# A Swin block with a dynamic convolution: channels in groups of 64, image halves on the partition halves, a written-out plan for the order

## The chip, the cores and the metric

The kernel runs on one core of one Trainium2 chip. A core has a matrix engine (TensorE, PE in the profile, with PEld for its weight loads), a vector engine (VectorE, DVE), a scalar engine (ScalarE, ACT), GpSimd (POOL) and SyncE (SP), which here only issues DMAs. Each takes its instructions in a fixed order and waits on semaphores. Work lies in SBUF, 128 partitions; products come out in PSUM, eight banks of 512 float32 a partition. The metric is the device time of one execution in microseconds, as the median of several runs.

## What is computed

Sixteen images of 192 channels and 56 x 56 pixels, all float32, go through a Swin block with shifted windows (7 x 7, shift 3, six heads of 32) and then through a depthwise 3 x 3 convolution whose taps are made from the image's own channel means. The reference, cut:

```python
# layer 0
h = _ln(transpose(x, (0, 2, 3, 1)), norm1_g, norm1_b)
h = roll(h, (-SHIFT, -SHIFT), axis=(1, 2))
win = windows of 7 x 7 tokens of h                       # 64 an image, N = 49 tokens
qkv = win @ qkv_w + qkv_b                                # q scaled by HD ** -0.5
attn = softmax(q @ k.T + bias + mask)                    # by head; the mask at the image's rim
out = (attn @ v) @ proj_w + proj_b
x1 = x + roll(windows put back, (SHIFT, SHIFT))
y = gelu(_ln(x1, norm2_g, norm2_b) @ fc1_w + fc1_b) @ fc2_w + fc2_b
x2 = x1 + y
# layer 1
t = relu(batch_norm(x2.mean(axis=(2, 3)) @ w1.T))
wt = (t @ w2.T + b2) * MASK                              # four of nine taps stay, by image and channel
out = depthwise_conv3x3(x2, wt) + bias
```

## The kernel before, in words

**Layout.** Channels lie on partitions as two halves of 96 (`HF`), so an image is a tile [96, 2, 56, 56], double buffered. A product over 192 channels is two matmuls of 96 rows that add up in PSUM. Single PSUM banks come from a pool of four (`bank`), double ones from a pool of two (`banks`).

**Norms.** For a chunk of eight image rows (448 tokens, `CT`), `norm_first` (L231) multiplies x by a matrix of ones over 192 on TensorE to get the mean on every partition (L238, `n_m`), subtracts it on VectorE (L241) and squares on ScalarE (L243). `norm_second` gets the variance as a second product (L250, `n_v`), the root on ScalarE (L252), the reciprocal on VectorE (L253), the product with x on GpSimd (L255), scale and shift on ScalarE (L257). The first norm of the next image runs beside the network of the present one and fills `xe`.

**Attention**, by rows of eight windows (392 tokens, `UT`). `windows` copies a row into window order on GpSimd (L286). `attention_qk` makes q and k in three products (L297: q of heads 0 to 3, k of heads 0 to 3, both of heads 4 and 5); k goes into block-diagonal tiles `kbd`, `kbd2`, zero outside of the blocks, so that one product gives the scores of four (or two) heads (L345, L352, `sc`). The softmax of four windows takes bias, maximum, subtraction on VectorE (L363 to L367), exp on ScalarE (L370), sum and reciprocal on VectorE (L372, L373), the product on GpSimd (L374, `prob`). `attention_v` makes v by window, once for even and once for odd heads (L390, `pv`; 49 columns of weights, at array column 0 or 64), and VectorE puts it into the block-diagonal `vbd` (L400). `attention_values` turns the probabilities on TensorE (L415, `pt`), copies them on ScalarE (L421, `prt`), multiplies (L426, `po`), projects (L445, `pp`) and adds to x on VectorE (L461).

**Network**, by chunks of 448 tokens: `mlp_first` (L470, `ph`; Gelu on ScalarE, L477), `mlp_second` (L486, `pf`), whose VectorE sum with x (L494) also gives the sums for the means.

**Convolution**: `conv_weights` makes the taps, `conv` the four taps of 96 channels, one on ScalarE (L533) and three on VectorE (L545), and writes the result.

**Order.** Image after image: first the eight rows of windows, beside them the convolution of the image before, then seven chunks of network beside the next image's first norm. Inside of these stages a scheduler orders each engine's instructions.

Of the kernel before, what the change touches and what calls it, by code (L numbers as in the profile page):

```python
# [14 lines left out]
HF = 96  # channels of a half: x and all that is as wide lies as two halves of 96 partitions  # L15
# [5 lines left out]
UT = NWIN * N  # tokens of a row of windows  # L21
EXT = IMG + SHIFT
PW = 64 + N  # partitions of two windows (or heads), the second at 64
CR = 8  # image rows of a chunk of tokens
CT = CR * IMG
NCHUNK = IMG // CR
# [3 lines left out]
NTAP = 4  # of the masked 3x3 taps, those that are kept  # L30
SCALE = HD ** -0.5
EPS = 1e-5
MASKED = -3.0e38


@with_exitstack
def tile_swin_then_dynamic_conv(
# [28 lines left out]
    B = x.shape[0]  # L66
    ctx.enter_context(nc.allow_non_contiguous_dma(reason="parameters, once"))

    const = ctx.enter_context(tc.tile_pool(name="const", bufs=1))
    xpool = ctx.enter_context(tc.tile_pool(name="xpool", bufs=2))  # L70
    wide = ctx.enter_context(tc.tile_pool(name="wide", bufs=2))
    lnp = ctx.enter_context(tc.tile_pool(name="lnp", bufs=2))
    att = ctx.enter_context(tc.tile_pool(name="att", bufs=2))
    small = ctx.enter_context(tc.tile_pool(name="small", bufs=4))
    ps1 = ctx.enter_context(tc.tile_pool(name="ps1", bufs=4, space=bass.MemoryType.PSUM))
    ps2 = ctx.enter_context(tc.tile_pool(name="ps2", bufs=2, space=bass.MemoryType.PSUM))

    def bank(name):
        return ps1.tile([128, 512], F32, tag="bank", name=name)

    def banks(name):
        return ps2.tile([128, 2, 512], F32, tag="banks", name=name)

    def load_x(b):
        t = xpool.tile([HF, 2, IMG, IMG], F32, tag="x", name=f"x_{b}")
        for kc in range(2):
            nc.sync.dma_start(t[:, kc], x[b, kc * HF : (kc + 1) * HF])
        return t

# [1 line left out]
    ident = const.tile([128, 128], F32, tag="ident", name="ident")  # L91
    make_identity(nc, ident)
    ones = const.tile([HF, HF], F32, tag="ones", name="ones")
    nc.vector.memset(ones, 1.0 / DIM)
    eps_t = const.tile([128, 1], F32, tag="eps", name="eps_t")
    nc.vector.memset(eps_t, EPS)

    def halves(src, name):
        t = const.tile([HF, 2], F32, tag=name, name=name)
        nc.scalar.dma_start(t, src.rearrange("(k p) -> p k", p=HF))  # L100
        return t

    def column(src, n, name):
        t = const.tile([n, 1], F32, tag=name, name=name)
        nc.scalar.dma_start(t, src.rearrange("(p o) -> p o", o=1))
        return t

    g1, be1 = halves(norm1_g, "g1"), halves(norm1_b, "be1")
    g2, be2 = halves(norm2_g, "g2"), halves(norm2_b, "be2")
    pb, f2b = halves(proj_b, "pb"), halves(fc2_b, "f2b")  # L110
    cb = halves(conv_bias, "cb")

    # q and k come in three products: q of heads 0-3, k of heads 0-3, and q | k of heads 4-5.
    wqkv = const.tile([HF, 2, 3 * DIM], F32, tag="wqkv", name="wqkv")
    qkv_v = qkv_w.rearrange("(k p) n -> p k n", p=HF)
    for to, lo, n in (
        (0, 0, 128),
        (128, DIM, 128),
        (256, 128, 64),
        (320, DIM + 128, 64),  # L120
        (384, 2 * DIM, DIM),
    ):
        nc.scalar.dma_start(wqkv[:, :, to : to + n], qkv_v[:, :, lo : lo + n])
    wp = const.tile([128, 2, DIM], F32, tag="wp", name="wp")
    nc.scalar.dma_start(wp[:, 0, :], proj_w[0:128, :])
    nc.scalar.dma_start(wp[0:64, 1, :], proj_w[128:DIM, :])
    wf1 = const.tile([HF, 2, HID], F32, tag="wf1", name="wf1")
    nc.scalar.dma_start(wf1, fc1_w.rearrange("(k p) n -> p k n", p=HF))
    wf2 = const.tile([128, NFC, DIM], F32, tag="wf2", name="wf2")
    nc.scalar.dma_start(wf2, fc2_w.rearrange("(f p) n -> p f n", p=128))  # L130
    f1b = const.tile([128, NFC], F32, tag="f1b", name="f1b")
    nc.scalar.dma_start(f1b, fc1_b.rearrange("(f p) -> p f", p=128))

    qkb = const.tile([128, 3], F32, tag="qkb", name="qkb")
    for dst, lo, n in ((0, 0, 128), (1, DIM, 128)):
        nc.scalar.dma_start(
            qkb[0:n, dst : dst + 1], qkv_b[lo : lo + n].rearrange("(p o) -> p o", o=1)
        )
    for part in range(2):
        lo = part * DIM + 128  # L140
        nc.scalar.dma_start(
            qkb[part * 64 : part * 64 + 64, 2:3],
            qkv_b[lo : lo + 64].rearrange("(p o) -> p o", o=1),
        )
    qbs = const.tile([128, 2], F32, tag="qbs", name="qbs")
    nc.vector.tensor_scalar(qbs[:, 0:1], qkb[:, 0:1], SCALE, None, ALU.mult)
    nc.vector.tensor_scalar(qbs[0:64, 1:2], qkb[0:64, 2:3], SCALE, None, ALU.mult)

    # v's bias as a row: even heads for partitions 0.., odd ones for partitions 64..
    vb = const.tile([PW, HEADS // 2, HD], F32, tag="vb", name="vb")  # L150
    vb_src = qkv_b[2 * DIM : 3 * DIM].rearrange("(o h j d) -> o h j d", o=1, j=2, d=HD)
    for j in range(2):
        nc.gpsimd.dma_start(
            vb[j * 64 : j * 64 + N], vb_src[:, :, j, :].broadcast_to([N, HEADS // 2, HD])
        )

    # Relative position bias of a pair of windows [q, h, k], with the shift's masks: by row of
    # windows (last or not) and pair in it (last or not).
    rel_r = wide.tile([PW, N, HEADS], F32, tag="wide", name="rel_r")
    nc.vector.memset(rel_r, 0.0)  # L160
    mask_t = lnp.tile([PW, 2, 2, N], F32, tag="sq", name="mask_t")
    nc.scalar.dma_start(mask_t, win_mask)
    # Reversed, the keys of a query are its rows and columns in the table, from its own on.
    side = 2 * WS - 1
    for j in range(2):
        for yq in range(WS):
            q = j * 64 + yq * WS
            nc.sync.dma_start(
                rel_r[q : q + WS].rearrange("p (y x) h -> p y (x h)", y=WS),
                bass.AP(  # L170
                    rel_bias.tensor,
                    yq * side * HEADS,
                    [[HEADS, WS], [side * HEADS, WS], [1, WS * HEADS]],
                ),
            )
    bias_t = const.tile([PW, 2, 2, HEADS, N], F32, tag="bias_t", name="bias_t")
    rel_hk = rel_r[:, ::-1, :].rearrange("p k h -> p h k")
    for r in range(2):
        for e in range(2):
            cut = mask_t[:, r, e, :].rearrange("p (o k) -> p o k", o=1)  # L180
            nc.vector.tensor_tensor(
                bias_t[:, r, e], rel_hk, cut.broadcast_to([PW, HEADS, N]), ALU.add
            )

    # The second layer's small network, with its weights transposed.
    w1n = lnp.tile([RED, DIM], F32, tag="rs", name="w1n")
    nc.scalar.dma_start(w1n, w1)
    w2n = wide.tile([HF, 2, NTAP, RED], F32, tag="wide", name="w2n")
    w2v = w2.rearrange("(k p t) r -> k p t r", k=2, t=9)
    b2t = const.tile([HF, 2, NTAP], F32, tag="b2t", name="b2t")  # L190
    b2v = b2.rearrange("(k p t) -> k p t", k=2, t=9)
    for kc in range(2):
        nc.scalar.dma_start(w2n[:, kc], w2v[kc, :, 0:NTAP, :])
        nc.scalar.dma_start(b2t[:, kc], b2v[kc, :, 0:NTAP])
    w1t = const.tile([HF, 2, RED], F32, tag="w1t", name="w1t")
    w2t = const.tile([RED, 2, NTAP, HF], F32, tag="w2t", name="w2t")
    for kc in range(2):
        pt = bank(f"w1p_{kc}")
        nc.tensor.transpose(pt[:HF, :RED], w1n[:, kc * HF : (kc + 1) * HF], ident[:RED, :RED])
        nc.vector.tensor_copy(w1t[:, kc, :], pt[:HF, :RED])  # L200
        pt = bank(f"w2p_{kc}")
        for t in range(NTAP):
            nc.tensor.transpose(
                pt[:RED, t * HF : (t + 1) * HF], w2n[:, kc, t, :], ident[:HF, :HF]
            )
        nc.vector.tensor_copy(
            w2t[:, kc].rearrange("p t c -> p (t c)"), pt[:RED, : NTAP * HF]
        )
# [17 lines left out]
    for t in [kbd, kbd2, vbd] + prob:  # L226
        nc.gpsimd.memset(t, 0.0)
# [179 lines left out]
    def attention_values(b, u, xt):  # L407
# [46 lines left out]
        if first + WS > IMG:  # L454
            runs.append((IMG - first, WS, 0))
# [230 lines left out]
```

## Time and profile before

| | us |
|---|---|
| runs of the kernel before | 7340.72, 7382.33, 7485.24 |
| their median | 7382.33 |
| span of the profiled execution | 7461.3 |

The profiled execution lies 1.1% over the median. The page gives the busy time of each engine, the span in 40 slices (a digit is a busy share in tenths; the row PEclk is the clock that TensorE was granted, in tenths of full), the DMA queues, the chain of work that ended last, and the costliest groups of instructions. A row of groups reads: line, engine, operation, result<-inputs, shapes, count | busy time, mean ns of one | idle time of the engine just before them, and what ended it. A float32 product stands in it as two records for each matmul of the code. The span and the two engines beside TensorE that the change loads most:

```profile
DVE  4434444344444444444444443444434444344442
ACT  2241422414223142331423314233242331413313
POOL 2111111111111010110101111111011110111100
```

Each image is a stretch of some 464 us, in which about 295 us are attention and 170 us network; ACT's larger digits are the network's Gelu.

### The profile page before, as it was taken

To read this page: it belongs to the slowest core of one execution; us is meant where nothing else is said; L and a number is where in the kernel's file an instruction comes from. 1 tells how busy PE (TensorE), PEld (TensorE's weight loads), DVE (VectorE), ACT (ScalarE), POOL (GpSimd) and SP (SyncE) were. 2 spreads that over 40 slices of the span, in tenths; PEclk is the share of its full clock that TensorE was granted. 3 is DMA by queue.
4 is the path that set the end of the run, shared out by engine and by line. 5 is a ranking of instruction groups with operands and counts; after the bars stand their busy time and mean duration, and the time that the engine had idled before them with its cause. 6 is when DMAs were issued, how large, how long until landed. Compare 5 with 4: busy or idle time off the path is not lost.

```text
span 7461.3 us, 72447 instructions
## 1 busy us (share of the span) xinstructions
PE 6817.7 (91%) x30026; PEld 3549.4 (48%) x30026; DVE 3170.6 (42%) x5505; ACT 2282.5 (31%) x3394; POOL 1044.7 (14%) x1007
## 2 busy tenths in 40 slices
PE   6998989989899898999989989899898998989987
PEld 3445444454444544445444454544544445444443
DVE  4434444344444444444444443444434444344442
ACT  2241422414223142331423314233242331413313
POOL 2111111111111010110101111111011110111100
PEclk8796967869678696786967869587695876958768
DMA  1000000000000000000000000000000000000000
GB/s 38 1 1 26 1 27 1 1 26 1 26 1 2 25 0 27 1 7 20 0 27 1 7 20 0 27 1 7 20 0 26 1 7 20 0 26 1 7 7 13
DMA packets 14171, 83.92 MB, mean 11 GB/s; under 512 B 5603, under 2 KB 7492, under 8 KB 7698
## 3 DMA queue, kind: packets, MB, share of 16 engines
q1 hardware_dynamic: 7952, 77.19, 3.8%
q8 instruction: 236, 3.87, 0.2%
q10 hardware_dynamic: 5826, 2.06, 0.1%
q14 instruction: 93, 0.76, 0.0%
q0 software_dynamic: 64, 0.04, 0.0%
HBM read 40.74 MB, written 38.54 MB: 11 GB/s over the span
## 4 chain that ended last, share of the span: by engine, by line
PE 83%; DVE 7%; ACT 6%; POOL 2%; issue 1%; DMA 0%; ACTq 0%; DVEq 0%; POOLq 0%
PE ph L470 14%; PE pf L486 13%; PE pp L445 9%; PE sc L345 9%; PE pv L390 8%; PE po L426 6%; PE sc L352 5%; PE n_v L250 4%; PE pt L415 4%; PE n_m L238 3%; PE pq L297 3%; PE pk L297 3%; PE pe L297 2%; DVE vbd L400 2%; ACT prt L421 2%; DVE n_rs L253 1%
## 5 line engine op out<-in xcount | busy, mean ns | idle before, releaser
L253 DVE RECIPROCAL n_rs<-n_rs 96x448 f32<-96x448 f32 x224 | 648.0, 2926 | 1022.4 <-ACT n_rs L252 1021.9
L470 PE MATMUL ph<-yn,wf 96*128 96x448 f32 x2688 | 1043.4, 542 | 35.9 <-ACT yn L257 35.9
L486 PE MATMUL pf<-hid,wf 128*96 128x448 f32 x2688 | 1049.8, 539 | 1.6 <-DVE x L494 1.6
L426 PE MATMUL po<-prt,vbd 113*64 113x49 f32 x6144 | 537.9, 301 | 323.6 <-ACT prt L421 318.7
L470 PEld LDWEIGHTS ph<-yn,wf 96*128 96x128 f32 x2688 | 509.4, 190 | 553.6 <-issue 473.1
L255 POOL TENSOR_TENSOR n_xc<-n_xc,n_rs 96x896 f32<-96x896 f32 x224 | 466.1, 2081 | 2029.5 <-DVE n_rs L253 2029.5
L390 PE MATMUL pv<-wqkv,win 96*49 96x96 f32 x8192 | 723.6, 328 | 0.0
L345 PE MATMUL sc<-kbd,q 128*64 128x196 f32 (+1 forms) x2048 | 721.1, 444 | 1.7
L445 PE MATMUL pp<-o,wp 128*96 128x392 f32 (+1 forms) x1024 | 709.8, 817 | 0.0
L486 PEld LDWEIGHTS pf<-hid,wf 128*96 128x96 f32 x2688 | 437.8, 163 | 571.5 <-issue 565.3
L461 DVE SCALAR_TENSOR_TENSOR x<-pp,pb,x 96x371 f32<-96x371 f32 (+2 forms) x576 | 187.8, 387 | 1217.1 <-PE pp L445 1217.1
L426 PEld LDWEIGHTS po<-prt,vbd 113*64 113x64 f32 x6144 | 462.4, 204 | 447.3 <-ACT prt L421 432.4
L390 PEld LDWEIGHTS pv<-wqkv,win 96*49 96x49 f32 x8192 | 600.5, 172 | 91.9 <-issue 75.9
L477 ACT ACTIVATE hid<-ph,f1b 128x448 f32<-128x448 f32 x672 | 424.1, 633 | 590.5 <-PE ph L470 590.2
L400 DVE TENSOR_TENSOR vbd<-pv,vb 49x96 f32<-49x96 f32 x2048 | 522.3, 255 | 128.3 <-PE pv L390 92.0
L363 DVE TENSOR_TENSOR e<-sc,bias_t 113x588 f32<-113x588 f32 x256 | 197.3, 771 | 885.9 <-PE sc L352 885.9
L286 POOL COPY win<-xe 96x392 f32<-96x392 f32 x256 | 171.5, 691 | 2841.4 <-PE pv L390 2837.4
L374 POOL TENSOR_TENSOR prob<-e,tot 113x588 f32<-113x588 f32 x256 | 344.4, 1348 | 1345.5 <-DVE tot L373 1338.7
L370 ACT ACTIVATE e<-e 113x588 f32<-113x588 f32 x256 | 174.9, 689 | 1168.3 <-DVE e L367 1167.0
L415 PE MATMUL pt<-ident,prob 113*128 113x113 f32 x1536 | 371.1, 374 | 173.5 <-ACT kbd L324 69.2
L352 PE MATMUL sc<-kbd,q 64*64 64x98 f32 (+1 forms) x2048 | 476.7, 323 | 1.4 <-ACT kbd L324 1.4
L309 ACT ACTIVATE q<-pq,qbs 128x392 f32<-128x392 f32 x128 | 75.2, 588 | 1192.3 <-PE pq L297 1192.3
(74 smaller groups left out, 6633.6 us busy)
## 6 DMA issues: line engine op xcount, KB each, us to landing
x<-in_x_dram SPq DMA_DIRECT2D x32, 1176.0 KB
out_dram<-y SPq DMA_DIRECT2D x32, 1176.0 KB, 6.3
wf<-in_L_conv_fc_w_dram ACTq DMA_DIRECT2D x2, 576.0 KB, 5.3
rel_r<-in_L_conv_rel_bias_dram SPq DMA_DIRECT2D x14, 8.0 KB
wqkv<-in_L_conv_qkv_w_dram ACTq DMA_DIRECT2D x2, 96.0 KB
wqkv<-in_L_conv_qkv_w_dram ACTq DMA_DIRECT2D x1, 144.0 KB
w2n<-in_L_conv_w_dram ACTq DMA_DIRECT2D x2, 72.0 KB
wqkv<-in_L_conv_qkv_w_dram ACTq DMA_DIRECT2D x2, 48.0 KB, 2.2
```

Source lines behind the costliest of these rows:

```text
L253: nc.vector.reciprocal(rs, rs)
L255: nc.gpsimd.tensor_tensor(xc, xc, rb, ALU.mult)
L297: nc.tensor.matmul(pq[:, :UT], wqkv[:, kc, i * 128 : (i + 1) * 128], win[:, kc].rearrange("p w t -> p (w t)"), start=(kc == 0), stop=(kc = ...
L345: nc.tensor.matmul(sc[rows_, i, 0 : 4 * N], q4[:, cols], kbd[:, w].rearrange("p h t -> p (h t)"), start=True, stop=True,)
L352: nc.tensor.matmul(sc[rows_, i, 4 * N : 6 * N], q2[:, cols], kbd2[:, w].rearrange("p h t -> p (h t)"), start=True, stop=True,)
L390: nc.tensor.matmul(pv[j * 64 : j * 64 + N, i * HF : (i + 1) * HF], win[:, kc, half * 4 + i, :], wv[kc][:, :, j, :], start=(kc == 0), stop= ...
L400: nc.vector.tensor_tensor(vbd[p, half * 4 + i, :, j * HD : (j + 1) * HD], pv[p, i * HF : (i + 1) * HF].rearrange("p (h d) -> p h d", d=HD) ...
L415: nc.tensor.transpose(pt[:, hp * PW : (hp + 1) * PW], pr[:, pair % 2, 2 * hp : 2 * hp + 2, :].rearrange("p h k -> p (h k)"), ident[:PW, :PW],)
L426: nc.tensor.matmul(o[(hp % 2) * 64 : (hp % 2) * 64 + 64, w * N : (w + 1) * N], vbd[:, w, hp, :], prt[:, hp * PW + s * 64 : hp * PW + s * 6 ...
L445: nc.tensor.matmul(pp[:HF, m, :UT], wp[:n, kc, mc], t.rearrange("p r w c -> p (r w c)"), start=(kc == 0), stop=(kc == 1),)
L470: nc.tensor.matmul(ph[:, :CT], wf1[:, kc, f * 128 : (f + 1) * 128], yn[:, kc, :], start=(kc == 0), stop=(kc == 1),)
L486: nc.tensor.matmul(po[:HF, m, :CT], wf2[:, f, m * HF : (m + 1) * HF], hid[:, f, :], start=(f == 0), stop=(f == NFC - 1),)
```

## The change

The kernel is written anew; the reference computation stays.

**Layout.** Channels come in three groups of 64 (`G`), and the partition halves hold two halves of the image: image rows 3 to 30 on partitions 0 to 63, rows 31 to 55 and then 0 to 2 on 64 to 127. Three image tiles [128, 3, 29, 56] take turns. A **round** is one row of windows in each half: 784 tokens; an image has four (`NU`), all images 64 (`S`). A matmul names the part of the array that it uses (`tile_position`): the two halves as row tiles of 64 (q and k, first layer), as column tiles of 64 (second layer, projection of heads 0 to 3), or as four tiles of 64 x 64 (scores, values, the rest of the projection), eight of 64 x 32 (weighted values), four of 128 x 32 (statistics).

**Norms.** Scale and shift of both norms are folded into the weights once, at the start, and so is the subtraction of the mean. What stays by token is 1 over the deviation: x and its square are added over the three groups on GpSimd (`fold`), a product with `blk` gives mean and mean square (`deviations`), and ln and exp(-0.5 ln) on ScalarE take the place of root and reciprocal. The row goes through DRAM to all partitions (one DMA out, two DMAs back for each norm), and GpSimd multiplies (`scaled1` into window order, `scaled2`).

**Attention.** VectorE writes k twice with a mask instead of into blocks. The softmax works on three groups of 16 x 49: VectorE adds the bias and takes maximum, sum and reciprocal, GpSimd subtracts and multiplies, ScalarE takes exp. VectorE turns the probabilities in 32 x 32 blocks, and 24 DMAs a round, all issued by SP, set the blocks in place (`turn_shares`). v comes with all heads at once and is copied by ScalarE; the bias of v is folded into the projection's.

**Network**: as before on 784 tokens; ScalarE changes its function table twice a round.

**Order.** Every operation is recorded with its engine, a duration, and what it reads and writes (`Plan.add`). TensorE's operations stay as recorded; `Plan.order` sets the others by a list schedule with these durations (a DMA's issue counts 0.1, its landing 2 to 4), and the program is put out in that order, each engine waiting for what it needs. PSUM is four double banks in turn (`bank`).

```diff
@@ the order of TensorE's work
+    for r in range(-2, S + 2):
...
+        if has(r + 2) and r > -2:
+            statistics(0, r + 2)
+        if has(r):
+            scores(r)
+        if has(r - 1):
+            weighted(r - 1)
+        if has(r):
+            turn_shares()
+            values(r, (0,))
...
+        if has(r - 1):
+            projection(r - 1)
+            statistics(1, r - 1)
+        if has(r):
+            values(r, (1,))
+        if has(r - 2):
+            second_layer(r - 2, (0, 1))
...
+        if norms:
+            deviations(norms)
+        if has(r + 2):
+            scaled1(r + 2)
+        if has(r - 1):
+            scaled2(r - 1)
+        if has(r - 2):
+            second_layer(r - 2, (2,))
+        if has(r + 1):
+            queries_keys(r + 1)
...
+        if has(r - 1):
+            table("gelu_and_others")
+            first_layer(r - 1)
+            table("natural_log_exp_and_others")
...
+    with tc.manual_schedule():
+        for i in plan.order():
+            plan.ops[i][2]()
@@ statistics and deviations
+            def go(src=src, f=f):
+                nc.gpsimd.tensor_tensor(f, src[:, 0], src[:, 1], ALU.add)
+            def go2(src=src, f=f):
+                nc.gpsimd.tensor_tensor(f, f, src[:, 2], ALU.add)
+            add("POOL", 1.0, go, keys, [("f", n, k)])
+            add("POOL", 1.0, go2, keys + [("f", n, k)], [("f", n, k)])
...
+            for k in range(2):
+                for n in norms:
+                    for h in range(2):
+                        c = 64 * n + 32 * h
+                        nc.tensor.matmul(
+                            p[c : c + 32, k, 0:HT],
+                            blk,
+                            fold[:, n, k, h * HT : (h + 1) * HT],
+                            start=True,
+                            stop=True,
+                            tile_position=(0, c),
+                        )
+
...
+        def away():
+            lo, hi = 4 * norms[0], 4 * norms[-1] + 4
+            nc.sync.dma_start(d[lo:hi], rs[lanes][::16])
...
+        for n in norms:
+            for ab in range(2):
+                def go(n=n, ab=ab):
+                    src = dv[n, ab].rearrange("(o h) t -> o h t", o=1)
+                    nc.sync.dma_start(
+                        rb[n][P(ab)].rearrange("p (h t) -> p h t", h=2),
+                        src.broadcast_to([64, 2, HT]),
+                    )
+                add("SP", 0.1, go, [dk], [("rb", n, ab)], lag=2.2)
@@ a product in two row tiles (q, k; the first layer has wf1, xs2)
+                for g in range(G):
+                    for ab in range(2):
+                        nc.tensor.matmul(
+                            p[:, ab, 0:UT],
+                            lhs_qk(ab, g, i),
+                            d[P(ab), g, 0:UT],
+                            start=(g == 0),
+                            stop=(g == G - 1),
+                            tile_position=(64 * ab, 0),
+                        )
@@ the softmax of a group and the turn
+            def less(j=j, ev=ev):
+                nc.gpsimd.tensor_tensor(
+                    ev, ev, top[j].broadcast_to([128, 16, N]), ALU.subtract
+                )
...
+            def share(j=j, ev=ev):
+                nc.gpsimd.tensor_tensor(ev, ev, tot[j].broadcast_to([128, 16, N]), ALU.mult)
...
+                def turn(kb=kb, e=e, t=t):
+                    nc.vector.transpose(t[:, kb], e[:, :, kb * TL : (kb + 1) * TL])
+                add("DVE", 0.7, turn, [("e", j), "epad"], [("t", ti, kb)])
+            for kb in range(2):
+                for w in range(2):
+                    for qb in range(2):
+                        def go(kb=kb, w=w, qb=qb, t=t, j=j):
+                            n = TL if kb == 0 else N - TL
+                            to, of = 64 * w + TL * kb, 64 * w + TL * qb
+                            nc.sync.dma_start(pt_t[j][to : to + n, qb], t[of : of + n, kb])
@@ weighted values, second layer
+                            nc.tensor.matmul(
+                                p[lane : lane + TL, w, at : at + 64],
+                                v[P(w), ab, pair, h * HD : (h + 1) * HD],
+                                pt_t[j][P(w), :, slot, :],
+                                start=True,
+                                stop=True,
+                                tile_position=(64 * w, lane),
+                            )
...
+                for f in range(NFC):
+                    for ab in range(2):
+                        nc.tensor.matmul(
+                            p[P(ab), i, 0:UT],
+                            wf2[:, f, g * 64 : (g + 1) * 64],
+                            hid[:, f, ab],
+                            start=(f == 0),
+                            stop=(f == NFC - 1),
+                            tile_position=(0, 64 * ab),
+                        )
```

## The prediction

> **What bounds the kernel now.** I read the page from the top: busy shares, the 40 slices, the chain that ended last; then equal stretches of one image, the order of TensorE's work in time, and the costliest groups.
>
> ```profile
> span 7461.3 us, 72447 instructions
> ...
> PE 6817.7 (91%) x30026; PEld 3549.4 (48%) x30026; DVE 3170.6 (42%) x5505; ACT 2282.5 (31%) x3394; POOL 1044.7 (14%) x1007
> ...
> PEclk8796967869678696786967869587695876958768
> ...
> PE 83%; DVE 7%; ACT 6%; POOL 2%; issue 1%; DMA 0%; ACTq 0%; DVEq 0%; POOLq 0%
> ```
>
> TensorE is busy for 91% of the span and carries 83% of the chain; no other engine reaches half. But its clock is granted at 0.777 in the mean. The stretches of one image (columns: stretch, its length, busy PE, PEld, DVE, ACT, POOL with counts, clock, DMA) say where:
>
> ```profile
> 2990.00:3030.00 40.00, 36.78 (x183) 20.48 (x181) 14.26 (x35) 6.37 (x13) 3.86 (x4) 0.54 0.00 1
> ...
> 3150.00:3190.00 40.00, 40.00 (x108) 18.25 (x107) 16.81 (x14) 19.93 (x27) 10.17 (x10) 1.00 0.00 0
> ```
>
> The network runs at 1.00; attention, TensorE just as "busy", at 0.54: its clock is halved for most of it. Two products show what a busy TensorE gets done (columns: start, length, group):
>
> ```profile
> 3127.02 3.17 PE L470 MATMUL ph<-yn,wf 96*128 96x448 f32 x8
> 3130.03 3.17 PE L250 MATMUL n_v<-n_sq,ones 96*96 96x448 f32 x8
> ```
>
> ```profile
> 3057.22 0.91 PE L390 MATMUL pv<-wqkv,win 96*49 96x96 f32 x16
> 3057.96 0.50 PE L345 MATMUL sc<-kbd,q 128*64 128x196 f32 x2
> ```
>
> Each f32 product is two records (1344 `ph` in the code, x2688 in the profile): two passes. Eight `ph` passes of 448 columns take 3.01 us from start to start of the next group: 0.376 us each, **0.84 ns a column and pass** at full clock[...]. Sixteen `pv` passes of 96 columns take 0.74 us, 46 ns each; alone one would take 96 x 0.84 = 81. `pv` puts 49 columns of weights at array column 0 or 64 in turn, so the two column halves work at once.
>
> [...] row tiles and four or eight at once no row of this trace shows. [...] The clock record here holds 1.0 and 0.5 alone. [...] `prob` takes 1.17 us in the median and, once an image, beside the convolution (`y` L545, 3.37 us), this:
>
> ```profile
> 3348.41 4.16 POOL L374 TENSOR_TENSOR prob<-e,tot 113x588 f32<-113x588 f32 x1 [4.51 <-DVE tot L373]
> ```
>
> **The change, part by part.** The unit is now a round: one row of windows in each image half, 784 tokens; 16 x 4 = 64 rounds, plus two before and two after. PE per round, as passes x columns x 0.84 ns / tiles at once:
> - q and k: 36 x 392 / 2 row tiles = 5.9 us. First layer: 72 x 392 / 2 = 11.9. Second: 72 x 392 / 2 column tiles = 11.9.
> - values: 96 x 192 / 4 = 3.9. Projection: 24 x 196 / 4 + 24 x 196 / 2 = 3.0. Statistics: 16 x 196 / 4 = 0.7. Scores: 96 x 98 / 4 = 2.0.
> - weighted: 192 x 64 / 8 = 1.3 if eight tiles keep up; if starts can come no closer than the 40 ns that `pv` and `po` show with two tiles, 192 x 40 = 7.7. I take 2.2: 384 weight loads and passes at the 6 ns that separate the closest starts of two tiles in the trace.
>
> Sum 41.5 us a round, 2,656 us in all. If four and eight tiles do no better than two, values, scores, statistics and the narrow projection double (+7.6) and weighted is 7.7 (+5.5): 54.6. Lower end 40.6.
>
> What goes: the transposes of probabilities on PE (`pt` 371 us) with their copies (`prt`, 224 on ACT), the means over channels as products (`n_m`, `n_v`: 779; statistics is 42 now), the reciprocals and small copies of the next rows:
>
> ```profile
> L253 DVE RECIPROCAL n_rs<-n_rs 96x448 f32<-96x448 f32 x224 | 648.0, 2926 | 1022.4 <-ACT n_rs L252 1021.9
> L255 POOL TENSOR_TENSOR n_xc<-n_xc,n_rs 96x896 f32<-96x896 f32 x224 | 466.1, 2081 | 2029.5 <-DVE n_rs L253 2029.5
> ...
> L400 DVE TENSOR_TENSOR vbd<-pv,vb 49x96 f32<-49x96 f32 x2048 | 522.3, 255 | 128.3 <-PE pv L390 92.0
> L363 DVE TENSOR_TENSOR e<-sc,bias_t 113x588 f32<-113x588 f32 x256 | 197.3, 771 | 885.9 <-PE sc L352 885.9
> ...
> L374 POOL TENSOR_TENSOR prob<-e,tot 113x588 f32<-113x588 f32 x256 | 344.4, 1348 | 1345.5 <-DVE tot L373 1338.7
> ```
>
> The other engines per round, durations scaled by elements from these rows and their like:
> - DVE: three softmax groups of 784 elements (771 ns for 588 gives 0.98; two reductions of 0.96, a reciprocal of 0.22) 9.3; k's blocks 3.3; nine additions of the projection 3.1; second layer 1.8; convolution 4.5 x 0.98 = 4.4; statistics 0.4; six transposes of 512 elements, which no row shows: 0.67 each like a one-input operation of that size, bounds 0.3 and 1.4, so 4.0 (1.8 to 8.4). Sum 26.3.
> - ACT: Gelu 5.5, exponentials 2.6, q and k2 3.3, v and o 3.6, squares 2.3, statistics 1.3, two table loads of 1.28, convolution 1.8. Sum 23.
> - POOL: 2.0 ns an element (`prob`, 1174 for 588) to 2.3 (`n_xc`): six operations of 784 9.4 to 10.9, eight folds of 392 6.3 to 7.3, scalings 5.0 to 5.6. Sum 21 to 24.
> - SP: 24 DMAs of turned probabilities, five for the norms, some 4.5 others: 34, issued 0.3 to 0.5 us apart in the trace's start: 10 to 17.
>
> All lie under 41.5, so they cost only where PE waits. I follow one round from its first score. POOL's subtractions start when the third maximum is taken, at 4.8 us, and its order is then fixed: three subtractions, a share, four folds of norm 2, two shares, four folds of the coming norm 1: 15.7 to 18.2 us, to 20.5 to 23. The statistics product needs the last fold; PE reaches it after 2.0 + 2.2 + 3.9 + 3.0 + 7.9 (two thirds of the second layer) = 19 us. **PE waits 1.5 to 4 us there**; I take 2.5. Queued behind it stand the last third of the second layer, q and k, and the first layer. Second: from statistics to the first layer PE has 4.0 + 5.9 = 9.9 us of cover. The chain there is four small operations, 2.0 with hops, a DMA out, 2.6, two DMAs back, 3 (both landing about 2.2 as `wqkv` does), and one scaling of GpSimd, 0.8: 8.4. It fits if SP is free: on SP the DMA out stands behind up to 23 of the turned probabilities, which end about 24.5 us; just in time. I take 1. Third: in three rounds of four, six convolution steps exclude POOL by turns, at most 6 us, and POOL is late already: 1.5 in the mean.
>
> A round: 41.5 + 2.5 + 1 + 1.5 = 46.5. [...] 62 full rounds: 2,883. The ends: to the first layer of the first round parameters, two norms and one softmax lie bare, about 80; the last two rounds and the convolution (18 x 0.98 on VectorE, writes of 6.3) about 75. Sum 3,038 against the 7461 of the profiled execution; that lies 1% over the median of runs, 7382, so **3,010**.
>
> **Rivals.**
> - All waits are hidden: 41.5 x 62 + 155 = 2,730. For it: every other engine has 15 us to spare. Against: POOL's fixed order.
> - Four and eight tiles work like two (54.6), or [...] the clock halves: attention's 13 us then take 26, and 5 of the network 10. About 55 to 60 us a round: 3,500 to 3,900. For it: attention at 0.54 now.
> - Row halves don't overlap at all: q, k and first layer double (+17.8), values, scores and half the projection too (+7): 66 to 71 a round, 4,300 to 4,600. No row speaks on it.
> - **Slower than before:** SP's DMAs land one by one. 34 x 3.4 us is 116.6, the 7461 / 64 of now: from 3.4 us a DMA on SP is the bound and decides; at 4, 34 x 4 x 64 = 8,700. For it: small transfers here land in 2.2 to 7.7 us, and each waits on SP in order. Against: the instructions wait for the DMA eight before, so eight are in flight and even 7.7 us gives 33 a round.
>
> **The numbers.** Forecast 0.56; all hidden 0.14; two tiles or half clock 0.2; row halves in series 0.06; SP 0.03; no change worth the name 0.01. Range 2,720 to 3,700: it holds the first three but for the end of the third. About 2% is what a measurement here tells from no change. Faster 0.96, same 0.01, slower 0.03.
>
> **What would show it.** Right: PE busy about 90% of 3,000, clock 0.95 or more; first-layer passes starting 165 ns apart in the mean (329 if row halves are in series); 96 value passes within 4 us (8 with two tiles); the statistics product waiting for POOL's folds some 2.5 us, 64 times; `xs2` released by DMA shortly before the first layer. Wrong: PE below 80%, slices of 5 or 6 in the clock row, waits of PE on the turned probabilities or on SP.

## The result, and the profile after

The changed kernel takes **4033.7 us** in the median of four runs (4030.08 to 4042.67), the kernel before 7387.3 in the four runs of that comparison: a ratio of 0.5465, 95% interval 0.5442 to 0.5489. That is far faster, as forecast, but 34% over the predicted 3,010 and 9% over the top of the range. The profiled execution spans 4033.5 us.

The page of the kernel after, its span, busy shares, clock and chain of waits:

```profile
span 4033.5 us, 92760 instructions
...
PE 3006.3 (75%) x40405; PEld 1786.6 (44%) x40405; DVE 1702.7 (42%) x2868; ACT 1401.6 (35%) x1884; POOL 1563.6 (39%) x1427
...
PEclk9888988988988988989889889889889888889888
...
PE 53%; DMA 23%; SPq 9%; DVE 6%; issue 6%; POOL 2%; ACT 1%; DVEq 0%; ACTq 0%; POOLq 0%
```

TensorE is busy for about 3,000 us and idle for 1,000, and it carries 53% of the chain instead of 83%. DMA and SP's queue, nearly absent before, carry 32%. The clock row is 8 and 9 throughout, without the fives and sixes of attention before. Which wait it is, the list of TensorE's waits says (engine, who waited, for what: us in all, times, longest):

```profile
PE ps L738 <- POOL xs L418: 815.7, 64, 18.1
PE ps L656 <- issue: 86.8, 66, 2.4
PE ps L314 <- POOL fold L300: 32.3, 6, 22.2
```

The first layer (L738) waits for the scaling of norm 2 (`xs`, L418) in every one of the 64 rounds, 815.7 / 64 = **12.7 us** in the mean. The statistics product (L314) waits six times in all. One round, in the timeline of TensorE (start, length, group, and the idle time ahead of it):

```profile
1998.34 2.25 PE L508 MATMUL ps<-kbd,q 64*64 64x98 f32 x96
2000.52 1.26 PE L656 MATMUL ps<-pt,v 64*32 64x64 f32 x71
2001.95 1.51 PE L656 MATMUL ps<-pt,v 64*32 64x64 f32 x121 [0.17 <-issue]
2003.40 0.55 PE L619 MATMUL ps<-wqkv,xs 64*64 64x192 f32 x7
2005.42 1.95 PE L619 MATMUL ps<-wqkv,xs 64*64 64x192 f32 x41 [1.48 <-issue]
2007.11 1.26 PE L687 MATMUL ps<-o,wp 64*64 64x196 f32 x24
2008.29 2.21 PE L701 MATMUL ps<-o,wp 128*64 128x196 f32 x24
2010.43 2.18 PE L619 MATMUL ps<-wqkv,xs 64*64 64x192 f32 x48
2012.55 8.12 PE L764 MATMUL ps<-hid,wf 128*64 128x392 f32 x48
2020.60 0.87 PE L314 MATMUL ps<-fold,blk 128*32 128x196 f32 x16
2021.40 4.17 PE L764 MATMUL ps<-hid,wf 128*64 128x392 f32 x24
2025.50 6.20 PE L433 MATMUL ps<-xs,wqkv 64*128 64x392 f32 x36
2043.05 13.92 PE L738 MATMUL ps<-xs,wf 64*128 64x392 f32 x72 [11.35 <-POOL xs L418]
```

From scores to the end of q and k everything runs nearly without a gap: 33.4 us. Then comes the hole of 11.4 us, and the first layer after it takes 13.9 us instead of 11.9: the clock record shows half clock from 2036.5 to 2046.7, and until then pairs of passes start about 0.65 us apart, 0.33 us afterwards. Second layer, q and k and scores take what the prediction gave them to within 0.3 us.

The chain of waits through the same hole (start, length, what; short pieces left out):

```profile
2021.35 0.63 DVE t L579
...
2022.04 0.55 SPq L587
...
2025.87 0.56 SPq L587
...
2026.48 6.70 DMA pt<-t
...
2033.25 4.91 DMA rsd<-rs
...
2038.20 0.67 SPq L369
...
2038.91 2.94 DMA rb<-rsd
...
2041.99 1.02 POOL xs L418
...
2043.05 13.92 PE ps L738 x72
```

Norm 2's factor `rs` (ScalarE, L351, started at 2024.5, 0.37 us) was ready at **2024.85**. Its DMA out (`rsd<-rs`) was issued at 2033.25, **8.4 us later**: on SP it stood behind 23 of the 24 DMAs of turned probabilities (L587, median 588 ns of SP's time each, about 0.62 from start to start). Ten of them were still to be issued when the factor was ready. Near the end SP also stopped twice, 1.5 us in all, until earlier DMAs had landed, because in this program a DMA's semaphore is used again by the eighth DMA after it; the last such landing, which the DMA out itself awaited, came 6.70 us after its issue. The DMA out then took 4.91 until SP could go on, the DMAs back 2.94. From `rs` to the scaling 17.1 us, where the prediction had 5.6 with a free SP.

Of the four kinds of rounds in an image two are like this one. In the other two the DMA out stands behind 15 or 19 of the 24 and starts after 3.5 or 4.9 us, but then the DMAs back are held up longer. In all four the time from `rs` to the scaling is 16.8 to 17.5 us in the mean.

### The profile page after: what moved, and what is told of

It reads as the page before. It is cut to its first block, busy times and chain, and to the rows that moved or that the text cites. A ratio compares the mean times of both kernels' runs of the same rounds, so it can differ in the third digit from the quotient of the medians.

```text
span 4033.5 us, 92760 instructions
## 1 busy us (share of the span) xinstructions
PE 3006.3 (75%) x40405; PEld 1786.6 (44%) x40405; DVE 1702.7 (42%) x2868; ACT 1401.6 (35%) x1884; POOL 1563.6 (39%) x1427
## 3 DMA queue, kind: packets, MB, share of 16 engines
q1 hardware_dynamic: 150722, 185.24, 17.5%
## 4 chain that ended last, share of the span: by engine, by line
PE 53%; DMA 23%; SPq 9%; DVE 6%; issue 6%; POOL 2%; ACT 1%; DVEq 0%; ACTq 0%; POOLq 0%
PE ps L738 23%; DMA pt<-t 12%; PE ps L764 11%; SPq L587 7%; PE ps L619 7%; DMA rb<-rsd 6%; PE ps L656 4%; DMA rsd<-rs 4%; PE ps L508 3%; PE ps L701 3%; DVE y L886 2%; DVE t L579 2%; POOL xs L418 2%; PE ps L687 1%; SPq L369 1%
## 5 line engine op out<-in xcount | busy, mean ns | idle before, releaser
L738 PE MATMUL ps<-xs,wf 64*128 64x392 f32 x4608 | 914.7, 560 | 815.7 <-POOL xs L418 815.7
L738 PEld LDWEIGHTS ps<-xs,wf 64*128 64x128 f32 x4608 | 499.6, 216 | 1230.9 <-POOL xs L418 905.7
L764 PE MATMUL ps<-hid,wf 128*64 128x392 f32 x4608 | 786.4, 495 | 0.0
L750 ACT ACTIVATE hid<-ps,b1f 128x784 f32<-128x784 f32 x384 | 350.6, 913 | 1107.8 <-PE ps L738 1105.1
L549 POOL TENSOR_TENSOR e<-e,top 128x784 f32<-128x784 f32 x192 | 296.8, 1575 | 863.1 <-DVE top L544 863.1
L418 POOL TENSOR_TENSOR xs<-x,rb 128x392 f32<-128x392 f32 x192 | 188.9, 1011 | 1084.9 <-DMA rb<-rsd 1084.9
L764 PEld LDWEIGHTS ps<-hid,wf 128*64 128x64 f32 x4608 | 319.5, 137 | 418.0 <-issue 399.7
L886 DVE SCALAR_TENSOR_TENSOR y<-x,wt,y 128x770 f32<-128x770 f32 x288 | 365.8, 1297 | 270.1 <-ACT y L862 258.4
L567 POOL TENSOR_TENSOR e<-e,tot 128x784 f32<-128x784 f32 x192 | 308.1, 1616 | 260.4 <-DVE tot L562 258.3
L433 PE MATMUL ps<-xs,wqkv 64*128 64x392 f32 x2304 | 398.3, 497 | 5.9 <-POOL xs L400 5.9
L619 PE MATMUL ps<-wqkv,xs 64*64 64x192 f32 x6144 | 313.0, 344 | 28.0 <-issue 28.0
L579 DVE STREAM_TRANSPOSE t<-e 128x512 f32<-128x512 f32 x384 | 254.2, 690 | 66.1 <-DMA pt<-t 60.1
L389 POOL TENSOR_TENSOR xs<-x,rb 128x343 f32<-128x343 f32 x192 | 184.6, 989 | 17.9 <-DMA rb<-rsd 17.9
```

Of the source, the lines that this page charges most:

```text
L418: nc.gpsimd.tensor_tensor(xs2[:, g], xv[:, g], rb[1], ALU.mult)
L433: nc.tensor.matmul(p[:, ab, 0:UT], lhs_qk(ab, g, i), d[P(ab), g, 0:UT], start=(g == 0), stop=(g == G - 1), tile_position=(64 * ab, 0),)
L549: nc.gpsimd.tensor_tensor(ev, ev, top[j].broadcast_to([128, 16, N]), ALU.subtract)
L567: nc.gpsimd.tensor_tensor(ev, ev, tot[j].broadcast_to([128, 16, N]), ALU.mult)
L579: nc.vector.transpose(t[:, kb], e[:, :, kb * TL : (kb + 1) * TL])
L619: nc.tensor.matmul(p[P(w % 2), ab, i * DIM : (i + 1) * DIM], d[P(ab), g, w * N : w * N + 64], wqkv[P(ab), g, 2 * DIM :], start=(g == 0), s ...
```

## The experiments

The variants ran in three batches (A, B, C), each beside the kernel before, whose median was 7373 us in A, 7483 in B and 7478 in C, and 7387 beside the kernel after. Small differences between batches are therefore read from the ratios. The column "wait" is the sum of the list's line for L738 behind L418, over 64 rounds.

| kernel | us, median (lowest to highest) | ratio, 95% interval | wait per round |
|---|---|---|---|
| after | 4033.7 (4030 to 4043) | 0.5465 (0.5442 to 0.5489) | 12.7 |
| transfers of 32 rows (A) | 3789.3 (3786 to 3794) | 0.5126 (0.5092 to 0.5161) | 8.8 |
| norm's DMAs on GpSimd (A) | 3658.4 (3642 to 3665) | 0.4948 (0.4917 to 0.4978) | 5.3 |
| both (B) | 3347.5 (3344 to 3351) | 0.4480 (0.4467 to 0.4493) | 2.2 |
| plan with SP at 0.6 us (A) | 3611.6 (3609 to 3618) | 0.4889 (0.4861 to 0.4917) | 5.4 |
| 32 rows and that plan (B) | 3478.6 (3475 to 3483) | 0.4655 (0.4642 to 0.4669) | 3.7 |
| 32 rows, only norm 2 on GpSimd (B) | 3845.7 (3840 to 3857) | 0.5152 (0.5133 to 0.5170) | 9.7 |
| that, and SP at 0.6 in the plan (B) | 3354.0 (3347 to 3363) | 0.4489 (0.4474 to 0.4504) | 2.4 |
| both, and SP at 0.6 in the plan (C) | 3338.0 (3335 to 3345) | 0.4474 (0.4449 to 0.4499) | 2.5 |
| no wait for norm 2 (A) | 3400.3 (3391 to 3409) | 0.4602 (0.4573 to 0.4630) | none |
| both, no wait for norm 2 (C) | 3169.9 (3164 to 3179) | 0.4248 (0.4224 to 0.4273) | none |
| both, weighted products twice (C) | 3749.1 (3742 to 3752) | 0.5020 (0.4986 to 0.5054) | 2.5 |

**Transfers of 32 rows.** Half of the turned probabilities' DMAs move 17 partitions, the rest of a block of 49. Here all move 32; the 15 more rows are padding.

```diff
-                            n = TL if kb == 0 else N - TL
+                            n = TL
```

> The 12 DMAs a round that move 17 rows of turned probabilities move 32 (the 15 further rows are zeros). Three theories on the 12.7 us that TensorE waits a round before the first layer. QUEUE: the norm's row stands on SP behind the turned probabilities, at 0.62 us an issue; the count of DMAs stays, so 4,030, within 1%. ONE ENGINE: a transfer of 17 rows runs on one DMA engine packet by packet and holds back the eighth row of the norm's transfer and the semaphores that SP waits for; with 32 rows the turned probabilities land in about 3 us instead of 6.7, the norm's row in 2.3 instead of 4.4; 4 us a round: 3,780 (3,700 to 3,850). CHAIN: the chain is long by itself and nothing in the queue matters: 4,030.

It gained 244 us although it moves more bytes, as ONE ENGINE had it. What a 17-row transfer does, the DMA row of the kernel after shows (2015 to 2045 us in 40 slices of 0.75 us: busy share of the 16 engines in tenths, then GB/s):

```profile
DMA  0543000000145410113441000000000005553000
GB/s 22 134 101 93 11 16 22 8 22 19 35 128 148 118 27 16 44 41 98 115 128 44 27 25 25 26 34 25 25 26 25 22 11 128 131 170 95 0 0 0
```

For nine slices, 2031.5 to 2038, data flow at 25 GB/s with a busy share below a tenth: packets of 2,048 bytes, 84 ns each, one after the other (2048 / 84 = 24.4 GB/s). That is 89 packets by 2038.7, those of several 17-row transfers, no two less than 80 ns apart: as from one engine of the sixteen, the same for all; the trace doesn't number them. Of the eight packets of the norm's DMA out, issued at 2033.25, seven go at 2034.5 to 2034.8 and the eighth at 2037.5, among them. The kernel with 32 rows has no such stretch in the round looked at: while SP issues its 24 transfers (1887.5 to 1905 us), 13 of 16 slices of 1.1 us carry 60 to 119 GB/s. Why 17 rows go packet by packet and 32 don't, no run shows. With 32 rows the time from DMA out to the first DMA back fell from 5.0 to about 2.0 us in rounds without convolution. In the mean of all rounds the time from `rs` to the scaling fell from 17.1 to 13.2 us: the DMA out starts 0.8 us sooner, the first DMA back follows it 2.2 sooner, and the scaling that one 1.0 sooner.

**The norm's DMAs on GpSimd.** The five DMAs of each norm go out on GpSimd's own queue instead of SP's.

```diff
-            nc.sync.dma_start(d[lo:hi], rs[lanes][::16])
+            nc.gpsimd.dma_start(d[lo:hi], rs[lanes][::16])
...
-        add("SP", 0.1, away, ["rs"], [dk], lag=2.0)
+        add("POOL", 1.0, away, ["rs"], [dk], lag=2.0)
...
-                    nc.sync.dma_start(
+                    nc.gpsimd.dma_start(
                         rb[n][P(ab)].rearrange(
...
-                add("SP", 0.1, go, [dk], [("rb", n, ab)], lag=2.2)
+                add("POOL", 1.0, go, [dk], [("rb", n, ab)], lag=2.2)
```

> The five DMAs of the norms go from SP's queue to GpSimd's. QUEUE: the DMA out starts within 1 us of the exponential instead of 3.4 to 8.8 later, and its two way back no longer wait on SP: some 7 of 12.7 us a round go, 3,550 (3,450 to 3,650). ONE ENGINE alone: the start was not what was late, the landing of the norm's eighth row stays over 4 us: a gain of 2 us a round at most, 3,900. CHAIN: 3,950 or more, and more yet by GpSimd's own issue of 0.9 us each.

375 us gained, just short of QUEUE's range. The DMA out starts 0.3 to 0.4 us after the exponential in nearly all rounds, in place of 3.4 to 9.3. The DMAs back still land late, 5.9 to 7.8 us from the first one's issue to the scaling, beside the 17-row transfers. The list's wait fell by 815.7 - 337.6 = 478 us, so 103 didn't reach the end: among other waits, scores wait 41.2 us for Gelu, which was no entry before, and TensorE's busy time at half clock rose from 341 to 428 us. Recording the DMAs on GpSimd also lets the plan order the other operations anew, here and in each variant that moves them; no run keeps that order fixed.

**Both together.**

> The 32 rows of e1 and the norms' DMAs on GpSimd's queue of e2 together. If QUEUE and ONE ENGINE are two separate causes that add up, the gains of e1 (244) and e2 (375) do too: 3,415. If they are two halves of one wait (SP late because its semaphores are late), e2 has most of e1's gain already: 3,570 to 3,640. CHAIN, in what is left: the first layer still waits, 3 us a round or more.

686 us, more than 244 and 375 added, and faster than every forecast. (By the ratios, which take out the batch, it is more too: 0.448 where the two gains added give 0.461.) The wait of the first layer and the chain of waits of one round:

```profile
PE ps L738 <- POOL xs L418: 138.8, 61, 10.5
```

```profile
1680.05 0.47 ACT m L344
...
1680.54 0.38 ACT rs L351
...
1681.20 1.70 DMA rsd<-rs
...
1683.19 0.63 POOL rb L369
1683.81 3.01 DMA rb<-rsd
...
1686.96 1.02 POOL xs L418
...
1688.02 0.93 PE ps L738 x4
```

From the factor to the scaling it is 6.0 us in this round, 6.7 in the mean, not far from the 5.6 of the prediction. And the page:

```profile
PE 2956.7 (88%) x40405; PEld 1750.3 (52%) x40405; DVE 1706.3 (51%) x2868; ACT 1399.8 (42%) x1884; POOL 1747.8 (52%) x1750
...
PEclk9899999999999999999999999999998999999987
```

The clock comes back with it: the record's half clock falls from 14.2 to 3.1 us a round, idle time included. What counts is the time in which TensorE works at half clock: 341 us in the kernel after, 366 with 32 rows, 428 with the norm's DMAs on GpSimd, 187 with both. Half of it is lost, and each cure alone leaves waits of 8.8 and 5.3 us that still halve the clock. That is large enough for the surplus of 67 us; no run separates it.

**A truer plan.** Only recorded numbers change: 0.6 us for each DMA on SP (0.1 before), and 3.0 for 2.5 for the landing of a turned block. (The two other landing times that the expectation names stayed at 2.0 and 2.2.) No DMA is moved to another engine, none changes its size; the list schedule alone orders them anew.

```diff
-        add("SP", 0.1, away, ["rs"], [dk], lag=2.0)
+        add("SP", 0.6, away, ["rs"], [dk], lag=2.0)
...
-                            0.1,
+                            0.6,
                             go,
                             [("t", ti, kb), "ptz"],
...
-                            lag=2.5,
+                            lag=3.0,
```

> Only the plan's durations are changed: 0.6 instead of 0.1 for each DMA that SP issues, 3.0, 2.5 and 3.0 us to landing instead of 2.5, 2.0 and 2.2. In the order that comes out the norm's DMA stands before ten of the turned probabilities' DMAs in most rounds (before one in the kernel after). QUEUE: four to six us a round go: 3,700 (3,600 to 3,800). ONE ENGINE: the landings are as slow as before, semaphores still late: 3,950. CHAIN: 4,030.

422 us gained without touching an instruction's work: the DMA out now stands ahead of 10 to 19 of the 24 transfers and starts 0.5 to 2.2 us after the exponential. With 32 rows as well:

> The 32 rows and the plan's durations of e5, all on SP. ONE ENGINE: in e5 the norm's row still took 3.3 to 4.0 us to land and the two back 3.6 to 6.2; with 32 rows 2.1 and 3.5: 2 to 3 us a round off, 3,610 to 3,450. QUEUE alone: 3,600.

3479, as ONE ENGINE had it: the 17-row transfers cost time with the better order too, and the wait falls from 5.4 to 3.7 us.

**Only norm 2 on GpSimd.** Norm 1 has more time, so its two DMAs back were left on SP, to save GpSimd's issues.

> As e4, but the two DMAs of norm 1 stay on SP, so that GpSimd issues three instead of five before the second norm's scaling. In e2 the scaling started 4.9 to 6.7 us after the first DMA back was issued, where SP's took 3.5 to 3.7. If the two further issues of about a us each on GpSimd's own queue are the difference: 2 us a round below e4, 130 us less. If it is the slower landing of GpSimd's transfers, the same as e4.

A miss: it gains nothing over the 32 rows alone (ratios 0.5152 and 0.5126, whose intervals overlap). The list of GpSimd's waits shows a new line.

```profile
POOL xs L389 <- DMA rb<-rsd: 540.5, 63, 12.0
```

In this order two of norm 1's scalings (L389) stand ahead of norm 2's on GpSimd, and they wait for DMAs behind 24 transfers on SP. SP's queue is back in the path through GpSimd's order. With 0.6 us in the plan for what is left on SP, norm 2's scaling stands first again:

> e6 with 0.6 for SP's issues in the plan. Aim: the version that beats both. The chain from the exponential to the scaling is then some 7 us under a cover of 10: the wait before the first layer falls under 3 us a round; 3,350 (3,250 to 3,450). If the convolution's output DMAs then hold up ScalarE, as they did in e3 (11 us once an image before a first-layer product), it ends at 3,400 or over.

That took the time to 3354. The same plan on the kernel with both cures:

> Both cures (32-row transfers, the norm's five DMAs on GpSimd's queue) and, in the plan, 0.6 us instead of 0.1 for a DMA on SP. QUEUE: once the norm's chain is off SP, a truer SP duration changes only where the 24 transfers stand in the plan; the wait before the first layer stays 2 to 2.5 us a round: 3,300 to 3,360. Rival PLAN: the order was wrong for the other engines too, the wait goes to 1 us: 3,250 to 3,290.

3338, which can't be told from both cures alone (3347, in another batch; the intervals of the ratios overlap), and the wait is no shorter. Once all of the norm is off SP the plan's figure for SP matters little.

**No wait for norm 2.** The scaling multiplies by a constant instead of the row, so nothing waits for the row's way through DRAM. This leaves out norm 2's division by the deviation.

```diff
-                nc.gpsimd.tensor_tensor(xs2[:, g], xv[:, g], rb[1], ALU.mult)
-            add("POOL", 1.05, go, X(s) + RB(1), [("xs2", g)])
+                nc.gpsimd.tensor_tensor(
+                    xs2[:, g], xv[:, g], wf2.rearrange("p f n -> p (f n)")[:, 0:UT], ALU.mult
+                )
+            add("POOL", 1.05, go, X(s) + ["wf2"], [("xs2", g)])
```

> The second norm's scaling takes a constant tile in place of the row that comes back by DMA; the DMAs stay. All three theories: the wait before the first layer goes, 12.7 us and some 2 us of half clock after it, 64 times 14.7 is 940: 3,090 (3,000 to 3,200). If the sum of the prediction was wrong elsewhere too (folds on GpSimd, tiles in fours, SP by itself), another wait takes its place and it stays over 3,300.

It missed by 310 us. Of the four kinds of rounds in an image two take 46 us, the predicted period; the others 52 and 61, with new waits of TensorE, and one of ScalarE behind the longest. Lines here stand two further down than in the kernel after (L740 is the first layer, L658 the weighted product, L864 the convolution's step); the lists of TensorE's and of ScalarE's waits:

```profile
PE ps L740 <- ACT hid L752: 170.4, 15, 12.5
...
PE ps L658 <- DMA pt<-t: 73.2, 18, 6.4
...
PE ps L658 <- DMA x<-in_x_dram: 28.4, 8, 7.2
```

```profile
ACT y L864 <- DMA out_dram<-y: 238.9, 36, 13.9
```

The convolution's step on ScalarE (`y`) waits for the writes of the result, and Gelu (`hid`) stands behind it. The three waits are 272 us; before, the second was 8.6 and the other two no entries. So most of 3,400 less 3,090 is waits that took the place of the one removed. On top of both cures they are nearly gone:

> Both cures, and norm 2's scaling does not wait for its row (it multiplies by a constant; the division by the deviation of norm 2 is left out of the result). Shows what of the wait before the first layer is left after the cures. QUEUE: the 2.2 us a round and the half clock it brings go, about 3 us x 62 = 190: 3,160, unless ScalarE's convolution step stands in front of Gelu again as in the run without norm 2's wait: then 3,250 to 3,400. RIVAL (the wait before the first layer was never the price; it only moves): 3,340 to 3,400, as much idle on TensorE as with both cures.

3170, 178 us below both cures: 2.9 us a round for what is left of the wait and its half clock, and the first layer's wait for Gelu is down to one of 3.3 us.

**Weighted products twice.** On top of both cures each weighted product is issued twice.

> Both cures, and the 192 weighted products of a round are issued twice (the same results written again). FETCH: TensorE stops about 1.4 us a round in this group because instructions are used up faster than they are fetched (12.7 ns a product, 24.8 with its weight load not counted apart); then twice as many cost 192 x 12.7 ns = 2.4 us and at least another 1.4 to 2 us of stops: 3.8 to 4.4 us a round, 240 to 290 more than with both cures, 3,590 to 3,640. TILES: the stop is a single one per round at the change of the tiling, not at the fetch; then 2.4 us a round, 150 more: 3,500.

It costs 402 us, 6.3 a round, more than either theory. The instruction queue and the group's stops, first with both cures, then in this run:

```profile
q8 instruction: 318, 5.21, 0.7%
...
PE ps L656 <- issue: 77.8, 59, 2.4
```

```profile
q8 instruction: 414, 6.78, 0.8%
...
PE ps L656 <- issue: 275.7, 159, 3.8
```

The instruction queue fetched 96 more packets of 16 KB; 24,576 more instructions / 96 = 256 a packet. The stops inside of the group grew from 77.8 to 275.7 us, 3.1 a round, and from 59 to 159 in number, where its products account for 2.4 to 3.0; more half clock (5.8 us a round against 3.1) may be the rest. A single stop for each change of tiling doesn't fit. That the group runs out of instructions does, and the traces hold a second sign: in the kernel after, 64 of the 66 stops over 0.4 us inside of the group end 1.2 to 1.6 us after a packet of the instruction queue had landed, and in this run 153 of 165.

## Why the prediction missed

The period from first layer to first layer is 61.1 us over 62 rounds, against 46.5 predicted: 14.6 x 62 = 906 of the 995 us between 4033.5 and the sum of 3,038. The other 89 are the ends. The 61.1 are 43.5 of products at full clock, 3.0 that the half clock adds to them, 12.8 of wait before the first layer and 1.8 of stops for instructions. Against the prediction the wait and its half clock are 14.8 too long. The 4.0 us charged to the statistics product and the convolution, which are no waits of their own here, happen to make up for the 3.8 that it lacked in products and stops; that is luck.

- **The step that failed: "Second: ... just in time. I take 1".** The wait before the first layer is 12.7 us and brings half clock. The prediction saw the place, the queue and the 23 DMAs ahead. It took 8.4 for the chain "if SP is free" under 9.9 of cover, then priced the unfree SP at 1. In the round shown the cover is 10.3, but the chain 21.6: 3.5 from the product to `rs`, 17.1 to the scaling, 1.0 for one scaling. Two terms were wrong. SP's turn: the 23rd DMA was issued 34 us after the first score, not by 24.5. SP takes 0.62 us for one, not 0.3 to 0.5, which makes 14 us of 23; it stood 2.4 us waiting for a turned block, and 1.5 for earlier landings, one of which came 6.7 us after its issue instead of about 2.2. The landings: the norm's own row took 4.9 to 5.0 where nothing else delayed it, because one of its eight packets went 2.7 us after the other seven, among those of 17-row transfers. Moving the queue alone gives 375 us, the rows alone 244, both 686; the wait that stays is 2.2 us. Even then the chain is no 8.4: 3.5 and 6.7 us and the scaling, 11 in all.
- **TensorE, 41.5 us.** Its products took 43.5 at full clock (from start to start of passes, gaps over 0.35 us left out): first layer 12.0, second 12.1 and q and k 5.9 as predicted; values 4.3 for 3.9, weighted 2.8 for 2.2, projection 3.4 for 3.0. A first-layer pass starts every 164 ns at full clock (165 forecast), 48 value passes take 2.18 us. Row tiles, four and eight tiles, whose overlap was an assumption of the prediction, do overlap; the rivals that had them in series fall. The stops for instructions, 1.8 us, were no term.
- **The other engines.** Their sums held: 26.6 us a round for VectorE (26.3 forecast), 21.9 for ScalarE (23), 24.4 for GpSimd (21 to 24). What failed is not the amount of their work.
- **The statistics product's wait, 2.5.** It is 32.3 us in six waits, all in the first 124 us of the run, so nothing in a full round; with both cures much the same (34.2). GpSimd's order came out as forecast, but the product doesn't wait for the last four of its eight folds: those belong to the product of the next round. The four of norm 2 had ended at 2016.8 in the round shown, 3.8 us ahead of it.
- **Convolution, 1.5.** Rounds come in kinds of 59.2, 60.1, 62.7 and 62.4 us, 1.9 above the shortest in the mean. That is near 1.5, but no run separates what the convolution costs GpSimd from the other work of these rounds. That it costs something the trace shows: GpSimd's product `e` (L567) took 2.15 us in the median beside a convolution step of VectorE (L886), 15 times, and 1.52 with VectorE idle.
- **Clock.** No half clock was priced, and there was some in every run (granted clock 0.878 to 0.978 in the kernel after and its variants). In the clock record of the kernel after, each of the 161 stretches of 1.0 or 0.5 ahead of the last is one to fourteen times 3.41 us long. In nine kernels (the one after and those of the table that keep norm 2's wait, but for the doubled products) half clock began during the wait before the first layer or within 3.5 us of its end in 399 of 400 rounds with a wait over 3.4 us, in none of 79 with a wait under 1 us, and in 40 of the 79 between. So a wait shorter than one such stretch was often enough. Waits of 12.7 us gave a clock of 0.882 in the mean, waits of 2.2 gave 0.964.
- **The ends, 155.** They took 144.6 to the first network and 99.5 from the last first layer but one to the end, 244 in all. The start's 80 forgot that the first network comes behind the scores of two rounds; its first layer also waited 14.6 us, those of the last two rounds 18.1 and 4.1.
- **The rivals.** The measured time lies in no rival's range: over that of two tiles or half clock (3,500 to 3,900), under that of row halves in series (4,300 to 4,600). The cause is the second half of the former, a clock halved by waits, but on the first layer rather than on attention. The rival of SP had the right queue and no sense of a middle: it asked whether SP's total of 34 DMAs bounds the round (about 20 us, it doesn't; its 34 x 3.4 is 115.6, a slip without effect), not where one urgent DMA stands in it. The range stopped at 3,700, 200 under the end of a rival, and no case was priced in which SP's order was late.
- **The signs.** PE below 80% came, as 75%, but the other two signs of being wrong did not: no 5 or 6 in the clock row, and TensorE waited only 8.6 us for turned probabilities. `xs` was released by the norm's DMA in every round, as for "right", only much later.

## What to carry to other kernels

A queue that is idle for most of a round (SP's issues take about 21 of 61 us here) can still cost it its longest wait (12.7 us): for each DMA on the critical chain, count what stands ahead of it in its queue at the moment its input is ready, with the issue time and the landings of those DMAs. Look at the row count of every transfer, for here transfers of 17 rows delayed what came after them more than transfers of 32 rows, by 244 us in all. And where a schedule is computed from recorded durations, a wrong one (0.1 us for 0.6) is a defect of the kernel like any other: correcting it alone gave 422 us here.

## What the runs showed of the hardware

- Transfers of more rows can delay what follows them less: with 32 instead of 17 rows in half of the turned probabilities' DMAs the norm's row took about 2.0 instead of 5.0 us from DMA out to first DMA back, and the kernel 244 us less, though it moved more bytes.
- TensorE stops for instructions. With eight tiles, the 192 passes of a round start 12.7 ns apart in the mean, stops left out, and the group stops about 1.3 us a round with "issue" as the only releaser. With both cures these stops are 77.8 us, with the products doubled 275.7, where the instruction queue fetched 96 more packets for 24,576 more instructions, 256 a packet. In the kernel after, 64 of its 66 stops over 0.4 us end 1.2 to 1.6 us after such a packet had landed.
- A DMA issued by GpSimd started 0.3 us after its input, and its issue took 601 ns of GpSimd's time, no less than SP's 592.
- Short waits can halve TensorE's clock: between 1 and 3.4 us, 40 of 79 did.
